# A two-layer decoder with divided tiles, and the score scale folded into the query weights

## Chip, core and metric

The kernel runs on one core of one Trainium2 chip. The metric is the device time of one execution in microseconds; the figure for a kernel is the median over its runs.

The engines are called as in the profile: PE (TensorE matmul; PEld is its weight load), DVE (VectorE), ACT (ScalarE), POOL (GpSimd) and SP (SyncE, which issues DMAs).

## What is computed

The input x is 64 sequences of 128 tokens of width 256, with a context of the same shape, all in float32. Two layers of three blocks each add to x; every block reads a layernorm of x:

```python
x = x + ssm(layernorm(x))                      # Mamba-like scan, convolution of 4, gate, rms norm
x = x + cross_attention(layernorm(x), ctx)     # 16 heads of 16, rotary, scale 0.25
x = x + recurrent_ffn(layernorm(x))            # c = f*c + i*g over the 64 sequences; tanh of x Wo + c_final Uo
x = x + self_attention(layernorm(x))           # rms norm, 16 query heads, 4 key heads, scale 1/16
x = x + wide_attention(layernorm(x), ctx)      # one head of 256, scale 1/16
x = x + experts(layernorm(x))                  # top 2 of 8 experts, and a shared expert
```

In each attention, `softmax(q k^T * scale) v`.

## The kernel before

**Tiling.** A group is G = 4 sequences, so T = 512 tokens; there are 16 groups. x stays in SBUF the whole time, one tile of 128 x 4 x 256 per group. The kernel has four stages, each with its own pools: stage 1 is the scan; stage 2 cross attention and the recurrence; stage 3 self attention, wide attention and routing; stage 4 the experts.

**Order.** Within a stage the work is written as Python generators, "tasks", with a start turn each. `run` advances every active task once per turn, oldest first, and a `yield` ends a task's turn. A group starts every 16 turns, an attention step (8 of the 16 heads of one sequence) every 2 turns. The tile framework then places the semaphores and fixes each engine's queue when the kernel is built. The trace shows that this queue isn't always in the order of the source: on DVE the instruction of L514 stands between those of L241 and L242.

**An attention step** (`heads`, L224 to L280). After two turns for the keys and values, two pairs of matmuls write the scores of 8 heads into a PSUM tile `s` (L236). DVE takes the maximum per head (L241) and multiplies it by minus the scale (L242), and ACT computes eight exponentials, `exp(scale*s - scale*max)`, into `e` (L245). Two turns later PE transposes the eight heads into a PSUM tile `pt` of two banks (L250). ACT copies the first four heads to `eT` (L252) and DVE the other four (L253). Two turns later the products with the values go to `av` (L261). Every second step ACT copies `av` out, PE transposes it back (L272), and DVE divides by the sums (L275, L277).

**Around it.** `block_diagonal` (L284, POOL) spreads the keys of four heads. `norm` computes the layernorm: statistics on DVE (L172 to L176), the power -0.5 on POOL (L163, `ln_rstd`) and the scaling on DVE (L189, `xn`). `transposed` (L200 to L204) transposes it through two PSUM tiles `pt_ln`; ACT copies the first half and DVE the second into one tile `xnT`. `project` (L211) and `project_rows` (L219) are the products with weights. In `cross_inputs` the rotary step writes `qT` and `kT` by halves (L512 to L519: PE, DVE, and two POOL instructions). The values `v` get a column block of ones from a POOL memset (L533, L669), so that the sums come out of the same product. The recurrence keeps its preactivations in `xg` (L577 to L607). `self_inputs` reads `xo` back from DRAM and adds it to x through POOL and ACT (L643 to L645). `route` writes its normalized, transposed x to DRAM (`XN`) for stage 4. POOL also scales some weights when they are loaded (`wout`, `fu`, `fuo`, `lwq`).

**PSUM in stages 2 and 3** (8 banks): three for `mm`, the tag of all short-lived products; two for `s`; two for `pt`; one for `av`.

The functions touched by the change, and what calls them:

Of the kernel before, what the change touches and what calls it, by code (L numbers as in the profile page):

```python
# [15 lines left out]
P = 128  # L16
# [46 lines left out]
def tile_decoder(ctx: ExitStack, tc: tile.TileContext, a: dict, out: bass.AP):  # L63
# [93 lines left out]
    nc.gpsimd.tensor_scalar_mul(fu, fu, 0.5)  # L157

# [35 lines left out]
    def transposed(work, ps, xn, bufs=2):  # L194

        xnT = work.tile([P, 2, T], F32, tag="xnT", name="xnT", bufs=bufs)
        for c in range(2):
            pt = ps.tile([P, T], F32, tag="mm", name="pt_ln")
            for b in range(G):
                nc.tensor.transpose(pt[:, b * P:(b + 1) * P], xn[:, b, c * P:(c + 1) * P], ident)  # L200
            if c == 0:
                nc.scalar.copy(xnT[:, c, :], pt)
            else:
                nc.vector.tensor_copy(xnT[:, c, :], pt)  # L204
        return xnT

    def project(ps, w, m0, m, rhs):

        o = ps.tile([P, T], F32, tag="mm", name="proj")
        for k in range(2):  # L210
            nc.tensor.matmul(  # L211
                o[:m, :], lhsT=w[:, k, m0:m0 + m], rhs=rhs[:, k, :], start=(k == 0), stop=(k == 1)
# [3 lines left out]
    def project_rows(dst, lhsT, w, b, m=None):  # L216

        for k in range(2):
            nc.tensor.matmul(  # L219
                dst, lhsT=lhsT[:, k, b * P:(b + 1) * P], rhs=w[:, k, :] if m is None else w[:, k, m],  # L220
# [3 lines left out]
    def heads(work, ps, b, c, state, q, kbd, v, scale):  # L224
# [9 lines left out]
        for hf in range(2):  # L234
# [4 lines left out]
            )  # L239
        mx = work.tile([P, 8], F32, tag="mx", name="mx", bufs=2)  # L240
        nc.vector.tensor_reduce(mx, s, AX.X, ALU.max)  # L241
        nc.vector.tensor_scalar(mx, mx, -scale, None, ALU.mult)  # L242
        e = work.tile([P, 8, P], F32, tag="e", name="e", bufs=2)
        for h in range(8):
            nc.scalar.activation(e[:, h, :], s[:, h, :], AF.Exp, bias=mx[:, h:h + 1], scale=scale)  # L245
        yield
        yield
        pt = ps.tile([P, 8, P], F32, tag="pt", name="pt")
        for h in range(8):
            nc.tensor.transpose(pt[:, h, :], e[:, h, :], ident)  # L250
        eT = work.tile([P, 8, P], F32, tag="eT", name="eT", bufs=2)
        nc.scalar.copy(eT[:, 0:4, :], pt[:, 0:4, :])  # L252
        nc.vector.tensor_copy(eT[:, 4:8, :], pt[:, 4:8, :])  # L253
# [6 lines left out]
        for vals, which, j, place in vh(c):  # L260
            nc.tensor.matmul(  # L261
                av[j * 32:j * 32 + 32, place, :], lhsT=vals, rhs=eT[:, which, :],
                start=True, stop=True,
            )
        if c == 1:
# [14 lines left out]
            state[b] = o  # L280

# [197 lines left out]
    for c in range(2):  # L479
        for w in (lwq, lwk, lwv):  # L480
            nc.gpsimd.tensor_scalar_mul(w[:, c, :], w[:, c, :], lg[:, c:c + 1])

# [7 lines left out]
    def cross_inputs(g, work, ps, got):  # L490
# [9 lines left out]
        for w, bias, src, tag in ((xwq, xbq, xnT, "qT"), (xwk, xbk, cT, "kT")):  # L500
            t = work.tile([P, 2, T], F32, tag=tag, name=tag, bufs=2)
# [8 lines left out]
            for c, raw in enumerate(raws):  # L510
                pr = ps.tile([P, T], F32, tag="mm", name="rot")
                nc.tensor.matmul(pr, lhsT=rot, rhs=raw, start=True, stop=True)  # L512
                tv = t[:, c, :].rearrange("p (b t) -> p b t", b=G)
# [6 lines left out]
            got[g, tag] = t  # L520
            yield
            yield
        got[g, "c"] = cT

    def cross_attention(g, b, c, work, ps, got):
        tb = slice(b * P, (b + 1) * P)

        def values():
            if c == 0:
                pv = ps.tile([P, T], F32, tag="mm", name="pv")  # L530
                project_rows(pv[:, :D], got[g, "c"], xwv, b)
                v = work.tile([P, 16, 32], F32, tag="v", name="v", bufs=3)
                nc.gpsimd.memset(v[:, :, 16:32], 1.0)  # L533
# [7 lines left out]
                (v[:, h, :], h % 8, h % 4, h // 4) for h in range(8 * c, 8 * c + 8)  # L541
# [3 lines left out]
            work, ps, b, c, got, got[g, "qT"][:, c, tb],  # L545
            lambda: block_diagonal(work, got[g, "kT"][:, c, tb]), values, 0.25,
# [18 lines left out]
    def recurrence(g, work, ps, got):  # L565
# [6 lines left out]
        xg = work.tile([P, 6, T], F32, tag="xg", name="xg")  # L572
        xo = work.tile([P, G, D], F32, tag="xo", name="xo")
        for part in range(2):
            for c in range(part * 3, part * 3 + 3):
                pp = project(ps, fx, c * P, P, xnT)
                nc.scalar.activation(xg[:, c, :], pp, AF.Identity, bias=fb[:, c:c + 1])  # L577
# [7 lines left out]
        for b in range(G):  # L585
            tb = slice(b * P, (b + 1) * P)
            c2 = got["c2"]
            for c0, n in ((0, 4), (4, 2)):
# [8 lines left out]
                pre = xg[:, c0:c0 + n, tb]  # L597
# [6 lines left out]
            nc.vector.scalar_tensor_tensor(kept, xg[:, 0:2, tb], 1.0, c2, ALU.add, ALU.mult)  # L604
            nc.vector.scalar_tensor_tensor(
                new, xg[:, 2:4, tb], 1.0, xg[:, 4:6, tb], ALU.add, ALU.mult
            )  # L607
# [600 lines left out]
```

## Time and profile before

| | |
|---|---|
| median of 3 runs | 3532.04 us (3531.86 to 3532.44) |
| profiled execution, its own time | 3483.77 us |
| its span | 3482.0 us |
| granted PE clock, mean | 0.948 |
| stage 1, to about | 784 us |
| stage 2, to about | 2000 us |
| stage 3, to about | 3050 us |
| one group in the steady part of stage 2 / stage 3 | 73 us / 57.6 us |

How to read the profile's lines. The trace is one execution. A line of a group gives source line, engine, operation, output and input with their shapes and the count; after the first bar the total busy time in us and the mean of one in ns; after the second bar the engine's idle time just before these instructions, with the engines and lines that ended it. A line of waits gives who waited for whom, the total in us, the number of times and the longest. A line of the timeline gives the start, the duration, the engine, and in brackets the idle time before it with what ended it. Idle time of an engine that doesn't bound the kernel costs nothing. The ends of PE's instructions are modelled, so a busy PE isn't necessarily a PE at its peak.

### The profile page before, as it was taken

The numbers are of one execution on the slowest core, as the hardware profiler recorded it, in microseconds if no ns is written. First come the engines' busy times: TensorE is split into PE (matmuls) and PEld (weight loads), VectorE is DVE, ScalarE is ACT, GpSimd is POOL, SyncE is SP. The second block draws the span as 40 slices with busy tenths as digits, with TensorE's granted clock in tenths as the row PEclk, the third lists the DMA queues.
The fourth block names the chain that finished last, engine by engine and source line by source line (L and its number), as shares of the span: only waits on it lengthen the run. The fifth ranks groups of instructions, "written<-read, shape, count | busy, mean of one in ns | idle before, by whom it ended". The sixth has DMA issues, their size and how long they took to land.

```text
span 3482.0 us, 48744 instructions
## 1 busy us (share of the span) xinstructions
PE 3176.3 (91%) x17486; PEld 2033.9 (58%) x17486; DVE 2273.2 (65%) x5498; ACT 1471.3 (42%) x3781; POOL 1302.8 (37%) x1290
## 2 busy tenths in 40 slices
PE   7899999998999999999999767999999999779989
PEld 4555555554666666666666633556566655468845
DVE  7999889965565556655565344777777777543355
ACT  3333333334545555455545234555555555213301
POOL 2444444455332323332332064233333333223276
PEclk9999999999999999999999878999998999789999
DMA  9980000001000000000000011101010101157655
GB/s 312 343 283 1 1 1 1 1 14 30 13 19 13 19 13 13 14 18 19 13 13 7 34 50 41 37 32 42 32 43 32 42 31 43 60 167 227 200 182 180
DMA packets 170658, 229.48 MB, mean 66 GB/s; under 512 B 19504, under 2 KB 142896, under 8 KB 170416
## 3 DMA queue, kind: packets, MB, share of 16 engines
q1 hardware_dynamic: 152448, 180.19, 16.0%
q0 software_dynamic: 17968, 46.18, 4.3%
q8 instruction: 138, 2.26, 0.3%
q14 instruction: 104, 0.85, 0.1%
HBM read 113.71 MB, written 127.93 MB: 69 GB/s over the span
## 4 chain that ended last, share of the span: by engine, by line
PE 62%; DVE 24%; POOL 6%; ACT 4%; DMA 2%; issue 2%; ACTq 0%; DVEq 0%; POOLq 0%; SPq 0%
PE proj L211 17%; PE pt L250 7%; PE s L236 6%; PE pu L593 5%; DVE acc L333 4%; DVE xn L189 4%; PE pgu L1019 4%; PE pv L219 3%; PE pt_ln L200 2%; PE av L261 2%; DVE mx L241 2%; PE pd L1028 2%; PE pxo L219 2%; PE pd L1079 1%; PE po L439 1%
## 5 line engine op out<-in xcount | busy, mean ns | idle before, releaser
L245 ACT ACTIVATE e<-s,mx 128x128 f32<-128x128 f32 x2048 | 555.9, 383 | 479.6 <-DVE mx L242 390.0
L284 POOL TENSOR_TENSOR kbd<-kT,consts 128x512 f32<-128x512 f32 x192 | 202.9, 1057 | 682.3 <-PE s L236 674.0
L253 DVE COPY eT<-pt 128x512 f32<-128x512 f32 x256 | 176.0, 687 | 392.7 <-ACT eT L252 391.7
L250 PE MATMUL pt<-consts,e 128*128 128x128 f32 x2048 | 362.5, 302 | 64.4 <-ACT e L245 62.6
L250 PEld LDWEIGHTS pt<-consts,e 128*128 128x128 f32 x2048 | 258.5, 148 | 180.8 <-ACT e L245 124.5
L211 PE MATMUL proj<-xnT,win 128*128 128x512 f32 x640 | 308.1, 621 | 48.9 <-DVE xc L323 45.0
L241 DVE TENSOR_REDUCE mx<-s 128x8 f32<-128x1024 f32 x256 | 310.5, 1213 | 10.0 <-PE s L236 9.9
L236 PE MATMUL s<-kbd,qT 64*128 64x512 f32 x1024 | 311.1, 686 | 1.5 <-POOL kbd L284 1.5
L252 ACT COPY eT<-pt 128x512 f32<-128x512 f32 x256 | 153.0, 598 | 191.7 <-PE pt L250 190.5
L211 PEld LDWEIGHTS proj<-xnT,win 128*128 128x128 f32 x640 | 119.9, 197 | 192.6 <-issue 112.6
L842 POOL DMA_INDIRECT xs<-xnr,r_rows x128 | 126.6, 989 | 271.5 <-DMA xs<-xnr,r_rows 183.8
L333 DVE SCALAR_TENSOR_TENSOR acc<-proj,convw,acc 128x508 f32<-128x508 f32 (+2 forms) x288 | 209.2, 730 | 7.7 <-ACT acc L329 6.2
L593 PEld LDWEIGHTS pu<-c,fu 128*128 128x128 f32 x1536 | 184.8, 196 | 24.9 <-issue 18.9
L593 PE MATMUL pu<-c,fu 128*128 128x128 f32 x1536 | 187.4, 280 | 8.9 <-DVE c L609 8.9
L392 POOL TENSOR_TENSOR ua<-consts,dt 128x1024 f32<-128x1024 f32 x64 | 121.9, 1906 | 179.7 <-DVE dt L366 150.6
L261 PE MATMUL av<-eT,v 128*32 128x128 f32 (+1 forms) x3072 | 174.5, 328 | 10.0 <-DVE eT L253 9.8
L211 PE MATMUL proj<-xnT,fx 128*128 128x512 f32 x384 | 173.4, 601 | 10.1 <-DVE v L534 9.6
L200 PE MATMUL pt_ln<-consts,xn 128*128 128x128 f32 x640 | 125.6, 316 | 61.5 <-DVE xn L189 39.5
L163 POOL TENSOR_TENSOR ln_rstd<-ln_ve,neghalf 128x4 f32<-128x4 f32 x96 | 98.0, 1021 | 210.4 <-DVE ln_ve L176 158.8
L189 DVE TENSOR_SCALAR xn<-x,ln_mv,ln_rstd 128x256 f32<-128x256 f32 x256 | 142.0, 600 | 40.4 <-POOL ln_rstd L163 40.4
L598 DVE TENSOR_TENSOR xg<-pu,xg 128x512 f32<-128x512 f32 (+1 forms) x128 | 71.4, 558 | 131.6 <-PE pu L593 131.6
L172 DVE BATCH_NORM_STATS2 ln_st<-x 128x6 f32<-128x256 f32 x384 | 146.3, 406 | 13.2 <-DMA x<-in_x_dram 6.2
(266 smaller groups left out, 6508.5 us busy)
## 6 DMA issues: line engine op xcount, KB each, us to landing
xs<-zeros SPq DMA_DIRECT2D x64, 1024.0 KB, 11.1
xs<-xs SPq DMA_DIRECT2D x71, 256.0 KB, 3.4
ys<-y SPq DMA_DIRECT2D x71, 256.0 KB, 2.3
ctxT<-in_ctxT_dram SPq DMA_DIRECT2D x32, 512.0 KB, 3.9
xo<-xo SPq DMA_DIRECT2D x32, 512.0 KB, 3.5
x<-in_x_dram SPq DMA_DIRECT2D x16, 512.0 KB, 8.9
xn<-xnT SPq DMA_DIRECT2D x16, 512.0 KB, 2.6
xnT<-xn SPq DMA_DIRECT2D x16, 512.0 KB, 4.6
```

Source lines behind the costliest of these rows:

```text
L189: nc.vector.tensor_scalar(xn[:, b, :], x[:, b, :], mv[:, b, 0:1], rstd[:, b:b + 1], ALU.subtract, ALU.mult)
L200: nc.tensor.transpose(pt[:, b * P:(b + 1) * P], xn[:, b, c * P:(c + 1) * P], ident)
L211: nc.tensor.matmul(o[:m, :], lhsT=w[:, k, m0:m0 + m], rhs=rhs[:, k, :], start=(k == 0), stop=(k == 1))
L236: nc.tensor.matmul(s[:, hf * 4:hf * 4 + 4, :], lhsT=q[rows], rhs=kb[rows, :, :], start=True, stop=True,)
L241: nc.vector.tensor_reduce(mx, s, AX.X, ALU.max)
L245: nc.scalar.activation(e[:, h, :], s[:, h, :], AF.Exp, bias=mx[:, h:h + 1], scale=scale)
L250: nc.tensor.transpose(pt[:, h, :], e[:, h, :], ident)
L253: nc.vector.tensor_copy(eT[:, 4:8, :], pt[:, 4:8, :])
L261: nc.tensor.matmul(av[j * 32:j * 32 + 32, place, :], lhsT=vals, rhs=eT[:, which, :], start=True, stop=True,)
L284: nc.gpsimd.tensor_tensor(out=kb, in0=mid(k, 4), in1=last(head, P), op=ALU.mult)
L333: nc.vector.scalar_tensor_tensor(acc[:, :, k:], pv[:, :, :P - k], convw[:, c, 3 - k:4 - k], acc[:, :, k:], ALU.mult, ALU.add,)
L593: nc.tensor.matmul(pu[:, i, :], lhsT=fu[:, k, c * P:(c + 1) * P], rhs=c2[:, k, :], start=(k == 0), stop=(k == 1),)
```

## The change

It has two parts.

1. **Tiles with two writers become two tiles.** `xnT`, `qT`, `kT` and `e`, `eT` are each split into two tiles; `pt` becomes two PSUM tiles of one bank, `pt0` and `pt1`; `xg` becomes a tile of 4 parts and one of 2. In `heads`, `tile_of` gives each head its place: heads 0, 1, 4, 5 go to the first tile and 2, 3, 6, 7 to the second, and the exponentials are issued in that order. The tiles `v` are allocated once (three in stage 2, two in stage 3), and the memset of their ones runs once each instead of once per sequence or group. `route` writes `xnT` with two DMAs instead of one.

2. **The scale and its sign move into weights.** POOL multiplies `xwq` and `xbq` by -0.25 and `lwq` by -1/16 once, when they are loaded. For the wide attention the ACT copies out of PSUM that produce `yu`, `ymb` and `ym` multiply by -1/16. The scores come out negated and scaled; the maximum becomes a minimum, used directly as the bias of `exp(-s + min)`. So the multiplications of L242 and L737 fall away.

The core of the diff:

```diff
     nc.gpsimd.tensor_scalar_mul(fu, fu, 0.5)
+    for w in (xwq, xbq):
+        nc.gpsimd.tensor_scalar_mul(w, w, -0.25)
...
-        xnT = work.tile([P, 2, T], F32, tag="xnT", name="xnT", bufs=bufs)
+        xnT = [work.tile([P, T], F32, tag=f"xnT{c}", name=f"xnT{c}", bufs=bufs) for c in range(2)]
...
         mx = work.tile([P, 8], F32, tag="mx", name="mx", bufs=2)
-        nc.vector.tensor_reduce(mx, s, AX.X, ALU.max)
-        nc.vector.tensor_scalar(mx, mx, -scale, None, ALU.mult)
-        e = work.tile([P, 8, P], F32, tag="e", name="e", bufs=2)
-        for h in range(8):
-            nc.scalar.activation(e[:, h, :], s[:, h, :], AF.Exp, bias=mx[:, h:h + 1], scale=scale)
-        yield
-        yield
-        pt = ps.tile([P, 8, P], F32, tag="pt", name="pt")
-        for h in range(8):
-            nc.tensor.transpose(pt[:, h, :], e[:, h, :], ident)
-        eT = work.tile([P, 8, P], F32, tag="eT", name="eT", bufs=2)
-        nc.scalar.copy(eT[:, 0:4, :], pt[:, 0:4, :])
-        nc.vector.tensor_copy(eT[:, 4:8, :], pt[:, 4:8, :])
+        nc.vector.tensor_reduce(mx, s, AX.X, ALU.min)
+
+        e, eT = (
+            [work.tile([P, 4, P], F32, tag=f"{n}{i}", name=f"{n}{i}", bufs=2) for i in range(2)]
+            for n in ("e", "eT")
+        )
+        for h in (0, 1, 4, 5, 2, 3, 6, 7):
+            i, at = tile_of(h)
+            nc.scalar.activation(
+                e[i][:, at, :], s[:, h, :], AF.Exp, bias=mx[:, h:h + 1], scale=-1.0
+            )
+        yield
+        yield
+        for i in range(2):
+            pt = ps.tile([P, 4, P], F32, tag=f"pt{i}", name=f"pt{i}")
+            for h in range(4):
+                nc.tensor.transpose(pt[:, h, :], e[i][:, h, :], ident)
+            if i == 0:
+                nc.scalar.copy(eT[i], pt)
+            else:
+                nc.vector.tensor_copy(eT[i], pt)
...
+    def tile_of(h):
+
+        return h % 4 // 2, h // 4 * 2 + h % 2
+
+    def values_of(work, n, i):
+
+        v = work.tile([P, n, 32], F32, tag=f"v{i}", name=f"v{i}")
+        nc.gpsimd.memset(v[:, :, 16:32], 1.0)
+        return v
...
+    nc.gpsimd.tensor_scalar_mul(lwq, lwq, -1.0 / 16)
...
-                v = work.tile([P, 16, 32], F32, tag="v", name="v", bufs=3)
-                nc.gpsimd.memset(v[:, :, 16:32], 1.0)
+                v = got["v"][(g * G + b) % 3]
...
-        xg = work.tile([P, 6, T], F32, tag="xg", name="xg")
+        xgs = [work.tile([P, n, T], F32, tag=f"xg{n}", name=f"xg{n}") for n in (4, 2)]
...
-        ps = PsumPool(psp, {"mm": 3, "s": 1, "pt": 1, "av": 1})
+        ps = PsumPool(psp, {"mm": 3, "s": 1, "pt0": 1, "pt1": 1, "av": 1})
...
-        nc.vector.tensor_reduce(mx, s, AX.X, ALU.max)
+        nc.vector.tensor_reduce(mx, s, AX.X, ALU.min)
 
         nc.vector.tensor_tensor(mx, mx, qb, ALU.add)
-        nc.vector.tensor_tensor(mx, qb, mx, ALU.subtract)
-        nc.vector.tensor_scalar(mx, mx, 1.0 / 16, None, ALU.mult)
+        nc.vector.tensor_tensor(mx, mx, qb, ALU.subtract)
...
-        nc.sync.dma_start(out=XN[g], in_=xnT)
+        for c in range(2):
+            nc.sync.dma_start(out=XN[g][:, c, :], in_=xnT[c])
...
-        nc.scalar.copy(yu, pb[:, :D + 1])
-        nc.scalar.copy(ymb, pb[:, D + 1:D + 3])
+        nc.scalar.mul(yu, pb[:, :D + 1], -1.0 / 16)
+        nc.scalar.mul(ymb, pb[:, D + 1:D + 3], -1.0 / 16)
...
-            nc.scalar.copy(ym[:, c, :], pw[:, :D])
+            nc.scalar.mul(ym[:, c, :], pw[:, :D], -1.0 / 16)
```

`qT`, `kT` and `xg` are divided in the same way, `halves` hands a whole tile on as a list of its two halves, and the pool of `work3` changes like that of `work2`.

## The prediction

> **What bounds the kernel now.** I read the page's busy shares first, then the stage windows, then who waits for whom on PE, and last the timeline of one loop period in each attention stage.
>
> ```profile
> PE 3176.3 (91%) x17486; PEld 2033.9 (58%) x17486; DVE 2273.2 (65%) x5498; ACT 1471.3 (42%) x3781; POOL 1302.8 (37%) x1290
> ```
>
> PE is busy 91% of the span, with 306 us idle. The change works mainly in stages 2 and 3, so their steady parts matter (columns: length, then busy time of PE, PEld, DVE, ACT, POOL; then granted clock, DMA share, GB/s):
>
> ```profile
> 870.00:1915.00 1045.00, 1004.88 (x6549) 656.36 (x6548) 613.91 (x1297) 536.67 (x1476) 336.41 (x326) 0.99 0.04 15
> 2176.00:2960.00 784.00, 749.94 (x4374) 468.50 (x4373) 584.74 (x1756) 410.75 (x1300) 256.94 (x279) 0.93 0.11 37
> ```
>
> PE is 96% busy in both. The whole pot is 40 us of PE idle in stage 2 (one group of four sequences takes 73 us, some 14 steady groups) and 34 us in stage 3 (57.6 us a group, some 14), plus matmuls stretched by a lower clock. PE's waits name their causes; first stage 2, then stage 3, steady part:
>
> ```profile
> PE pt_ln L200 <- DVE kT L514: 20.6, 14, 1.8
> PE proj L211 <- DVE v L534: 9.6, 11, 1.4
> PE pt L250 <- ACT e L245: 9.1, 13, 0.7
> ...
> PE pt L250 <- ACT e L245: 21.7, 16, 1.7
> ```
>
> So a wait comes about once per group and kind. By contrast, the largest waits that the change attacks sit on engines with slack:
>
> ```profile
> L245 ACT ACTIVATE e<-s,mx 128x128 f32<-128x128 f32 x2048 | 555.9, 383 | 479.6 <-DVE mx L242 390.0 <-DVE r_s L816 36.3 <-PE pr L557 33.3
> ...
> L253 DVE COPY eT<-pt 128x512 f32<-128x512 f32 x256 | 176.0, 687 | 392.7 <-ACT eT L252 391.7
> ...
> L242 DVE TENSOR_SCALAR mx<-mx 128x8 f32<-128x8 f32 x256 | 85.2, 333 | 2.7
> ```
>
> DVE's copy of its half of eT waits 392 us in all for ACT's copy of the other half, and the exponentials wait 390 us for L242. That is no gain as such: only what reaches PE counts. One stage 2 period shows how it does, first DVE's timeline, then ACT and PE:
>
> ```profile
> 1324.80 1.21 DVE L241 TENSOR_REDUCE mx<-s 128x8 f32<-128x1024 f32 x1
> 1325.94 0.67 DVE L514 TENSOR_TENSOR kT<-rot,consts 128x512 f32<-128x512 f32 x1
> 1326.54 0.76 DVE L242 TENSOR_SCALAR mx<-mx 128x8 f32<-128x8 f32 x1
> ```
>
> ```profile
> 1327.38 2.17 ACT L245 ACTIVATE e<-s,mx 128x128 f32<-128x128 f32 x8 [2.33 <-DVE mx L242]
> ...
> 1327.80 0.33 PE L250 MATMUL pt<-consts,e 128*128 128x128 f32 x1 [0.70 <-ACT e L245]
> ```
>
> The reduce is done at 1326.01, another group's kT comes between, L242 is stretched, and the exponentials start 1.37 us after the maxima were known. The queue's order isn't the source's: something was put between two lines that stand together. Stage 3's stall, on PE:
>
> ```profile
> 2443.55 2.13 PE L250 MATMUL pt<-consts,e 128*128 128x128 f32 x8 [1.39 <-ACT e L245]
> 2445.62 2.08 PE L236 MATMUL s<-kbd,qT 64*128 64x512 f32 x4
> ```
>
> L241 ended at 2442.84 there, L242 at 2443.04, and the exponentials began at 2443.13. After 1.39 us idle the eight transposes follow the exponentials one by one, and the scores take 2.08 us where other steps show 1.13.
>
> **What the Trainium skill says.** "TensorE: Matmul & The Clock Gate", Part 1: PE falls to half clock after an idle window of about 3.4 us. The trace agrees on the half: windows of 3.41 us from 2268.5 have clock 0.50. It doesn't agree that the window must be idle: PE was 2.70 of 3.41 us busy in the one before. "PSUM — Partial Sum Buffer", PSUM bank collisions: two engines must be kept apart in one bank, not in different banks. pt's halves lie in different banks, yet the trace shows DVE's copy starting at ACT's end, so the wait belongs to the shared tile, and separate tiles should free it. "SBUF — State Buffer", Who interferes with whom: a DVE tensor_scalar in its two-port mode and GpSimd exclude each other. L242 fits: median 170 ns, mean 333, longest 2304.
>
> **The change, part by part.** Gains are negative.
>
> *L242 goes (256 times, 85 us of DVE), with L737 (16 x 169 ns).* Stage 2: from 1326.67 to 1330.15 PE needs 3.48 us for 8 pt_ln, 8 pt and 2 pv. Undisturbed these advance by 0.92, 1.03 and 0.48 (other steps), 2.43 in all. The loss of 1.05 holds the 0.70 wait and the pace of the exponentials. With those at 1326.1 the loss is gone: 14 x 1.05 = -15. The waits for kT (1.44) and v (1.36) stay: L242 lies behind kT and v, not ahead. Stage 3: the exponentials could start at 2442.93 instead of 2443.13, but ACT's r_s at 2442.97, which waits for DVE too, may still stand ahead; of 0.2 I take 0.1. Less DVE work in this crowded stretch gives 0.2 more of the short waits after it (0.40 for r_sel, 0.27 for xnT): 14 x 0.3 = -4.
>
> *Clock.* 0.93 over 784 us means 14% of the time, 110 us, at half rate, which costs up to 55 us. Idle shrinks by 0.3 of the group's 2.2 us (14%; the 2.2 are 1.39 for e, the two short waits, and 0.14 for the wide attention's v), so -8. Stage 2: 0.99 costs at most 10; a third, -3. This term is the least sure: bounds 0 and -40 together.
>
> *e, eT and pt in two tiles each.* The eight exponentials, eight transposes and two copies remain. ACT's copy can start after four transposes (0.5 us sooner), DVE's at the eighth rather than after ACT's 0.58 us. av comes two turns later and waits for eT only 9.8 us in the span. Transposes already follow single exponentials, so dividing e gives nothing. In itself 0; DVE's copy leaving earlier is rival A.
>
> *xnT, qT, kT and xg divided.* L604 starts at 1311.94 while the second tanh on xg ends at 1312.49: parts of these tiles are already told apart. Bounds -3 and +3; 0.
>
> *v's memset (64 + 16 times, 0.31 us on POOL, waiting 143 us for av).* POOL's work behind it, kbd above all, waits for s anyway. v's DVE write takes over the wait, for reads of three sequences ago: done four turns before. Bounds -3 and +1; 0.
>
> *Weights scaled on POOL.* xwq is 128x512, like fuo's 1.54 us; xbq (128x2) is near dpar's 0.22 us. xwq lands at about 44 us (issued 34.6 to 36.1, 7.9 more), and POOL idles 15.4 us before 59.3. Hidden, unless queued ahead of the ua at 37.8: up to +6. lwq's 1.54 us falls at 794 to 802, where POOL runs without a break ahead of qT: +1.5. The wide attention's scale moves into ACT copies already there: 0.
>
> *route's DMA.* 16 more issues at 0.32 us on SP. XN is read in stage 4; SP is nearly idle: 0.
>
> *Ramps.* At 2029 to 2176 PE's exponential waits of 2 to 4 us come from the ring of xo (DMA 3.6, POOL 2.34, ACT 1.06, POOL 2.35), which isn't touched. Elsewhere about -3. Stages 1 and 4: no operation goes; 0.
>
> Sum: -15 - 4 - 8 - 3 + 1.5 - 3 = -31.5, taken as -32. The profiled execution has a span of 3482.0 and took 3483.8 us; the runs' median is 3532.0, 48 us more. I find nothing in the trace to split that 48, and carry the difference over: span 3450, median **3500**.
>
> **The rivals.** *A, eT's copy fills a hole.* DVE idles 1.06 us at 1321.1 and 1.13 us at 2438.6, waiting for POOL's ln_rstd, while eT is ready but for ACT. Its copy (0.60) then runs behind three xn. In the hole it would pull mx, kT and the exponentials 0.6 us ahead in both stages: (14 + 14 groups) x 0.6 = -17, and the clock gives 18 more, if a third of its 55 is tied to these stalls: 3500 - 35 = 3465. For it: on this chip the eighth transpose ends at 1321.45, in the hole. Against it: the order is fixed at build, and the copy would have to overtake three instructions, not one.
>
> *B, nothing reaches PE.* The stalls stay because DVE's other work (four xn, mx, kT) or ACT's r_s sets them, and only some 5 us come, from the ramps and the clock: 3527. The 0.70 wait, which has no cause but L242, speaks against it.
>
> *C, slower.* The new order puts DVE's eT copy, which needs the last transpose, ahead of work that frees a PSUM buffer, kT or v. All DVE work then stands behind it while PE is paced by the exponentials, about 2.2 us a period. 28 x 2.2 = +62, with 10 of clock: 3500 + 72 = 3572. It makes the change a loss from 32/28 = 1.1 us a group. For it: PE already waits for kT and v 27 times, so no slack is left there. Against it: the copy becomes ready earlier, not later.
>
> That the divided tiles free no wait is possible too; the sum has no gain from them, so it would end A and leave 3500.
>
> **How the numbers follow.** Forecast 0.52 (own range 3480 to 3520), A 0.23, B 0.10, C 0.15. Low takes in A with a better clock, 3445; high takes in B, the queued ua and a weak C, 3540. About 7 us, 0.2%, is what a measurement of this kernel can tell from no change: faster 0.75, same 0.10, slower 0.15.
>
> **What would show it.** Right: L242 gone and the exponentials waiting for L241; eT's DVE copy no longer waiting for ACT; PE's 9.1 us for e in stage 2 near zero while its 20.6 and 9.6 stay; stage 2 groups about 72 us; stage 3 clock 0.94 to 0.95. A: the waits for kT fall to half and the clock rises to 0.97. Wrong: a new wait on PE that recurs once a group, or a stage 1 that moves by more than 5 us.

## The result, and the profile after

| | before | changed |
|---|---|---|
| median of the runs | 3531.95 us (4 runs, 3530.0 to 3532.4) | 3503.61 us (4 runs, 3500.5 to 3511.0) |
| ratio | | 0.9924, 95% interval 0.9907 to 0.9941 |
| profiled execution, its own time | 3483.8 us | 3501.5 us |
| its span | 3482.0 us | 3499.7 us |

The changed kernel is 0.8% faster. The two profiled executions say the opposite, 3484 against 3501 us, so their spans can't be compared; parts of the kernel between fixed marks can. The marks are the starts of PE's first and last products with a weight (`xwq` opens stage 2, `fx` is the recurrence, `lwq` opens stage 3, `ym` is the wide attention), and of the last product with an expert's gate and up weights. A stage's ramp is the part before its groups come at a steady pace. In us:

| part | before | changed | difference |
|---|---|---|---|
| stage 1, to the first `xwq` | 791.6 | 792.5 | +0.9 |
| stage 2's ramp, to the first `fx` | 105.4 | 100.3 | -5.1 |
| stage 2, first to last `fx` | 1067.0 | 1052.2 | -14.8 |
| to the first `lwq` | 51.3 | 49.3 | -2.0 |
| stage 3's ramp, to the first `ym` | 140.9 | 125.8 | -15.1 |
| stage 3, first to last `ym` | 861.4 | 870.5 | +9.1 |
| to the last expert product | 287.3 | 289.0 | +1.7 |
| from there to the end | 177.1 | 220.1 | +43.0 |

Up to the last expert product the changed kernel gains 25.3 us, close to the 28 of the medians. The last row is a matter of the execution (experiment 0). The 0.9 us of stage 1 mean nothing: two executions of the kernel before differ by 4.5 us there (791.6 and 796.1). The ramp of stage 3 gains as much as all of stage 2, and the steady part of stage 3 loses.

The page's first line, and then the two stage windows, of the changed kernel:

```profile
PE 3183.3 (91%) x17486; PEld 2043.9 (58%) x17486; DVE 2233.7 (64%) x5226; ACT 1470.4 (42%) x3781; POOL 1286.1 (37%) x1218
```

```profile
870.00:1915.00 1045.00, 1016.99 (x6666) 663.51 (x6664) 594.42 (x1195) 549.67 (x1497) 316.05 (x267) 1.00 0.05 15
2176.00:2960.00 784.00, 753.33 (x4306) 474.05 (x4306) 567.12 (x1609) 405.28 (x1295) 254.94 (x265) 0.92 0.11 37
```

DVE has 272 instructions fewer (5498 before), which are the 256 of L242 and the 16 of L737, and POOL 72 fewer. In stage 2 PE is busy 1017 us of the 1045 instead of 1005, at clock 1.00 instead of 0.99, and it gets more done: 6666 products in the same 1045 us instead of 6549. In stage 3 the clock is 0.92 instead of 0.93, and the 784 us hold 4306 products instead of 4374 although PE is busy for longer. PE's waits, stage 2 first, then stage 3:

```profile
PE pt L263 <- ACT e L255: 14.0, 14, 2.8
PE proj L216 <- DVE v L558: 13.8, 13, 1.3
```

```profile
PE pt L263 <- ACT e L255: 30.3, 28, 2.1
```

In stage 2 the wait for kT, the largest of before (20.6 us), is gone; the waits for e and v remain and are larger than before (9.1 and 9.6). In stage 3 PE waits for e twice a group instead of once. But the waits of before for r_sel, eT and xnT (4.8, 3.1 and 1.7 us) shrink to 0.8 us for r_sel, so that all of PE's listed waits in stage 3 come to 31.6 us before and 31.4 after. The loss there isn't waiting. Part of it shows in the transposes of e, in the same window, first before, then changed (PE's busy time is the first number after the length, with its count):

```profile
2176.00:2960.00 784.00, 155.16 (x870) 113.09 (x870) 0.93 0.11 37
```

```profile
2176.00:2960.00 784.00, 165.09 (x856) 112.98 (x856) 0.92 0.11 37
```

That is 178 ns each before and 193 after, about 0.9 us for the 64 of a group: at the second stall they too follow the exponentials one by one, and the trace counts that as busy. The groups on the other engines:

```profile
L255 ACT ACTIVATE e<-s,mx 128x128 f32<-128x128 f32 x2048 | 557.4, 384 | 493.2 <-DVE mx L247 490.9
...
L267 DVE COPY eT<-pt 128x512 f32<-128x512 f32 x256 | 176.2, 688 | 337.3 <-PE pt L263 333.6
```

The exponentials now wait for the reduce itself (L247), and DVE's copy of eT for PE and no longer for ACT's copy. The timelines of DVE, ACT and PE in a stage 2 group, in that order:

```profile
1313.57 1.21 DVE L247 TENSOR_REDUCE mx<-s 128x8 f32<-128x1024 f32 x1
1314.71 1.27 DVE L539 TENSOR_TENSOR kT<-rot,consts 128x512 f32<-128x512 f32 x2
```

```profile
1314.88 2.18 ACT L255 ACTIVATE e<-s,mx 128x128 f32<-128x128 f32 x8 [3.97 <-DVE mx L247]
```

```profile
1313.79 0.64 PE L275 MATMUL av<-eT,v 128*32 128x128 f32 x16
1315.30 1.62 PE L263 MATMUL pt<-consts,e 128*128 128x128 f32 x6 [0.87 <-ACT e L255]
1316.76 0.27 PE L202 MATMUL pt_ln<-consts,xn 128*128 128x128 f32 x1
```

The exponentials start 0.10 us after the reduce ends (1314.78), where it was 1.37. And PE's own queue is another one. Before, two `pt_ln` stood ahead of the first transpose of e and waited 1.44 us for the PSUM buffer that kT held:

```profile
1326.67 0.44 PE L200 MATMUL pt_ln<-consts,xn 128*128 128x128 f32 x2 [1.44 <-DVE kT L514]
```

Now six transposes of e come first, and while they run kT is read. So the change has moved PE's order too, which is set when the kernel is built. With the scale alone (experiment 1) the six transposes stand first as well, with the tiles alone they don't: it is the instruction taken from DVE that changes the order on PE. The experiments ask which of these things pays.

### The profile page after: what moved, and what is told of

It is laid out like the page before. It is cut to its first block, busy times and chain, and to the rows that moved or that the text cites. A ratio compares the mean times of both kernels' runs of the same rounds, so it can differ in the third digit from the quotient of the medians.

```text
span 3499.7 us, 48489 instructions
## 1 busy us (share of the span) xinstructions
PE 3183.3 (91%) x17486; PEld 2043.9 (58%) x17486; DVE 2233.7 (64%) x5226; ACT 1470.4 (42%) x3781; POOL 1286.1 (37%) x1218
## 4 chain that ended last, share of the span: by engine, by line
PE 63%; DVE 22%; POOL 6%; issue 4%; DMA 2%; ACT 2%; another core or an unknown queue 1%; POOLq 0%; DVEq 0%; ACTq 0%; SPq 0%
PE proj L216 16%; PE pt L263 8%; PE s L241 6%; PE pu L619 5%; DVE acc L357 4%; PE pv L224 4%; DVE xn L191 3%; PE pgu L1046 3%; PE av L275 3%; PE pt_ln L202 3%; DVE mx L247 2%; PE pr L723 2%; PE pxo L224 2%; PE pd L1055 1%
## 5 line engine op out<-in xcount | busy, mean ns | idle before, releaser
L263 PEld LDWEIGHTS pt<-consts,e 128*128 128x128 f32 x2048 | 255.1, 147 | 192.8 <-ACT e L255 105.4
L216 PE MATMUL proj<-xnT,win 128*128 128x512 f32 x640 | 308.8, 622 | 48.1 <-DVE xc L347 45.1
L247 DVE TENSOR_REDUCE mx<-s 128x8 f32<-128x1024 f32 x256 | 311.9, 1219 | 62.5 <-PE s L241 61.9
L241 PE MATMUL s<-kbd,qT 64*128 64x512 f32 x1024 | 308.7, 681 | 1.2 <-POOL kbd L308 1.2
L265 ACT COPY eT<-pt 128x512 f32<-128x512 f32 x256 | 157.1, 614 | 119.0 <-PE pt L263 118.5
L216 PE MATMUL proj<-xnT,fx 128*128 128x512 f32 x384 | 172.3, 598 | 14.2 <-DVE v L558 13.8
L202 PE MATMUL pt_ln<-consts,xn 128*128 128x128 f32 x640 | 117.5, 320 | 43.5 <-DVE xn L191 42.5
L1070 POOL DMA_INDIRECT ys<-ys,t_yrow x128 | 123.8, 967 | 86.1 <-DVE x L1082 37.1
```

The source lines that it names most:

```text
L216: nc.tensor.matmul(o[:m, :], lhsT=w[:, k, m0:m0 + m], rhs=rhs[k], start=(k == 0), stop=(k == 1))
L241: nc.tensor.matmul(s[:, hf * 4:hf * 4 + 4, :], lhsT=q[rows], rhs=kb[rows, :, :], start=True, stop=True,)
L247: nc.vector.tensor_reduce(mx, s, AX.X, ALU.min)
L263: nc.tensor.transpose(pt[:, h, :], e[i][:, h, :], ident)
```

## The experiments

The stage times of all of them, as in the table above, in us ("sum" is from the first `xwq` to the last `ym`). Before's second profile agrees with its first within 0.8 us in all these parts but one, where it is 3.2 us off (and so is the sum); so differences of more than some 4 us in a part mean something although the totals scatter by 10 to 30. Each row is one profile. The ratios, not the medians, compare the kernels: each kernel ran beside runs of the kernel before, whose medians were 3533.7 to 3536.8 us in the experiments and 3532.0 in the result.

| kernel | ratio to before | stage 2 ramp | stage 2 | to `lwq` | stage 3 ramp | stage 3 | sum |
|---|---|---|---|---|---|---|---|
| before | 1 | 105.4 | 1067.0 | 51.3 | 140.9 | 861.4 | 2226.0 |
| 0 before again | | 105.7 | 1067.7 | 48.1 | 140.6 | 860.6 | 2222.7 |
| changed | 0.9924 | 100.3 | 1052.2 | 49.3 | 125.8 | 870.5 | 2198.1 |
| 1 scale only | 0.9909 | 102.3 | 1050.3 | 51.3 | 119.3 | 872.8 | 2196.0 |
| 2 tiles only | 0.9992 | 104.1 | 1061.1 | 51.3 | 139.2 | 863.3 | 2219.0 |
| 3 scale; e, eT, pt divided | 0.9945 | 100.5 | 1057.0 | 50.9 | 124.8 | 871.7 | 2204.9 |
| 4 changed; e, eT, pt whole | 0.9910 | 101.1 | 1048.5 | 49.5 | 120.4 | 872.1 | 2191.6 |
| 5 scale; x 1.0 in stage 3 | 0.9889 | 101.8 | 1052.4 | 49.6 | 118.5 | 866.1 | 2188.4 |
| 6 scale; x 1.0 aside | 0.9936 | 102.9 | 1050.9 | 49.4 | 120.1 | 872.6 | 2195.9 |
| 7 as 4; x 1.0 in stage 3 | 0.9896 | 101.2 | 1049.2 | 49.6 | 121.0 | 864.6 | 2185.6 |
| 8 scale; PE's order in stage 3 | 0.9936 | 101.4 | 1050.3 | 51.3 | 120.6 | 885.2 | 2208.8 |
| 9 scale; x 1.0 elsewhere | 1.0025 | 106.7 | 1066.7 | 48.1 | 140.0 | 864.9 | 2226.4 |
| 10 before; PE's order in stage 2 | 1.0051 | 106.0 | 1083.8 | 51.2 | 139.8 | 865.7 | 2246.5 |
| 11 as 4; PE's order in stage 3 | 0.9940 | 102.0 | 1048.3 | 49.6 | 119.4 | 883.4 | 2202.7 |

### 0. The kernel before, profiled again

No edit.

> The kernel before, unchanged, profiled once more. Its first profiled execution took 3483.8 us, its other runs 3532. Theory one, the 48 us lie in the tail: the experts end near 3300 us as they did (3299.8), and the part from there to the end takes about 230 us instead of 182. Theory two, they are spread over the stages: the experts end near 3345 us and the part after them takes about 182 us.

The time was 3539.4 us, and the last expert product fell at 3304.4 us (3304.9 in the first profile). Windows from about there to the end, first of before's first profile, then of its second:

```profile
3305.00:3482.00 177.00, 153.69 (x458) 87.22 (x456) 91.52 (x185) 18.27 (x31) 123.08 (x128) 0.96 0.59 180
```

```profile
3304.50:3537.50 233.00, 162.71 (x458) 92.88 (x456) 90.74 (x185) 18.05 (x31) 124.07 (x128) 0.86 0.44 137
```

The same 458 products and the same 128 gathers of experts' rows from DRAM took 177 and 233 us: in the second PE stands idle for 70 us instead of 23. Theory one holds: the 48 us that the prediction carried over lie in the output tail. The transfers themselves took no longer. The queue of the gathers, in the same two windows:

```profile
q0 software_dynamic: 6144, 16.79, 33.5%
```

```profile
q0 software_dynamic: 6144, 16.79, 24.6%
```

33.5% of 177 us are 59, and 24.6% of 233 are 57. So the added time lies between the transfers; what holds it up stays open. The changed kernel's profile has a tail of the usual kind (220 us; all profiles but before's first have 218 to 233).

### 1 and 2. The two halves of the change

The scale alone: in the kernel before, only the scaling in the weights and the minimum, with all tiles and memsets as they were (the wide attention's lines, changed likewise, are left out here).

```diff
+    for w in (xwq, xbq):
+        nc.gpsimd.tensor_scalar_mul(w, w, -0.25)
...
-        nc.vector.tensor_reduce(mx, s, AX.X, ALU.max)
-        nc.vector.tensor_scalar(mx, mx, -scale, None, ALU.mult)
+        nc.vector.tensor_reduce(mx, s, AX.X, ALU.min)
...
+    nc.gpsimd.tensor_scalar_mul(lwq, lwq, -1.0 / 16)
```

> The kernel before with only the scale moved into the weights (L242 and L737 go); every tile stays undivided and the memsets of v stay. Theory S, the removed DVE instruction carries the gain: 3505 to 3515 us, a stage 2 group at about 71.7 us instead of 72.95, and the experts end 15 to 25 us earlier. Theory T, the divided tiles carry it: 3525 to 3532 us, a stage 2 group within 0.3 us of 72.95.

The tiles alone are the changed kernel with these lines taken back:

> The changed kernel with the scale taken back (L242 and L737 are there again); all tiles are divided and v is static. Theory S: 3525 to 3535 us, a stage 2 group near 73 us. Theory T: 3500 to 3515 us, a stage 2 group near 71.7 us, and the wait of PE for kT gone as in the changed kernel. Both together: 3515 to 3520, each half of the 28 us.

Measured: the scale alone 3507.7 us, ratio 0.9909 (0.9891 to 0.9928); the tiles alone 3531.1 us, 0.9992 (0.9980 to 1.0005). Theory S holds in the total and in the place: the scale alone has the changed kernel's stage 2, its stage 3 ramp (somewhat shorter still) and its stage 3 loss. A group takes 71.71 us in stage 2 (median) and 58.8 in stage 3 (mean of ten groups), against 72.95 and 58.1 before; the 57.6 given for before at the top is too short for a mean. The tiles alone take 6 us off stage 2 and change each other part by 2 us or less. PE's waits in stage 2 of the scale alone, then of the tiles alone:

```profile
PE pt L251 <- ACT e L246: 18.8, 15, 1.7
PE proj L213 <- DVE v L536: 8.0, 13, 0.6
```

```profile
PE pt_ln L200 <- DVE kT L537: 16.0, 14, 2.9
PE pt L262 <- ACT e L254: 9.4, 14, 0.7
PE proj L214 <- DVE v L556: 8.3, 10, 0.9
```

The wait for kT goes with L242, not with the divided kT.

### 3 and 4. Which tiles

The scale, and of the tiles only e, eT and pt:

> The kernel before with the scale moved and only e, eT and pt divided; xnT, qT, kT and xg are whole and the memsets of v stay. If scale and attention tiles make the change, as both theories so far have it: 3500 to 3508 us, with stage 3's ramp near 126 us and a stage 3 group near 58.5 us as in the changed kernel. If the division of xnT, qT, kT and xg or the static v carries a part of it: 3515 us or more.

The opposite: the changed kernel with only these three made whole again.

```diff
-        for i in range(2):
-            pt = ps.tile([P, 4, P], F32, tag=f"pt{i}", name=f"pt{i}")
...
+        pt = ps.tile([P, 8, P], F32, tag="pt", name="pt")
+        for h in range(8):
+            nc.tensor.transpose(pt[:, h, :], e[:, h, :], ident)
+        eT = work.tile([P, 8, P], F32, tag="eT", name="eT", bufs=2)
```

> The changed kernel with e, eT and pt whole again; the scale in the weights, the divided xnT, qT, kT and xg and the static v stay. Stages 2 and 3 (first product with xwq to last with ym) took 2226.0 us before, 2198.1 in the changed kernel, 2196.0 with the scale alone, 2204.9 with the scale and divided e, eT, pt. If the effects add up, dividing e, eT and pt costs 9 us and the other divisions give 7: 2189 us here, and 3495 to 3500 in all. If dividing e, eT and pt is neutral and only moves PE's queue by chance: 2196 to 2200, and 3503 to 3508.

Measured: 3517.1 us, 0.9945 (0.9928 to 0.9961), so the other divisions carry a part; and 3500.7 us, 0.9910 (0.9895 to 0.9924), sum 2191.6 where 2189 was expected of effects that add up. They do, roughly, in the stages: with the other tiles whole, dividing e, eT and pt costs 8.9 us (2204.9 against 2196.0), with the others divided 6.5 (2198.1 against 2191.6); dividing the others and keeping v gives 4.4 to 6.8. These are sums from one profile each, which repeat to some 3 us, and in the totals the intervals of the changed kernel and of the one with e, eT and pt whole overlap. So the divided copy of eT, whose freed wait (392 us) is the largest that dividing tiles removes, brings nothing, and the three divided tiles together seem to cost a little. Why was not settled; in stage 2 the wait for v is larger with it (16.4 us against 8.0 in the scale alone).

### 5 and 6. The chain to the exponentials, or DVE's load

Experiment 6 puts DVE's 256 instructions back, but beside the chain; experiment 5 puts them into the chain in stage 3's steady groups alone.

```diff
         nc.vector.tensor_reduce(mx, s, AX.X, ALU.min)
+        side = work.tile([P, 8], F32, tag="side", name="side", bufs=2)
+        nc.vector.tensor_scalar(side, mx, 1.0, None, ALU.mult)
```

> The kernel with the scale alone, and at each step DVE multiplies the minima by 1.0 into a tile that nobody reads: as many DVE instructions as before, but none between the reduce and the exponentials. Theory chain: what counts is the shorter chain; stage 2 at 1050 to 1054 us, stage 3's ramp at 119 to 122, the total within 5 us of the scale alone. Theory load: DVE's 85 us of work count; stage 2 returns to 1060 or more, the total to within 10 us of the kernel before.

Measured: 3510.0 us, 0.9936 (0.9923 to 0.9948); stage 2 1050.9 us and the ramp 120.1, as without these instructions. The sum is 2195.9 us against 2196.0; the ratio is a little worse than that of the scale alone, with intervals that overlap (0.9891 to 0.9928). In the stages DVE's 85 us of work count for nothing; the place of L242 between the reduce and the exponentials is what counted. Experiment 5:

```diff
-    def heads(work, ps, b, c, state, q, kbd, v, scale):
+    def heads(work, ps, b, c, state, q, kbd, v, extra):
...
         nc.vector.tensor_reduce(mx, s, AX.X, ALU.min)
+        if extra:
+            nc.vector.tensor_scalar(mx, mx, 1.0, None, ALU.mult)
```

`extra` is true for `g >= 2` in `self_attention`, false in stage 2.

> The kernel with the scale alone, and in stage 3 from the third group on DVE multiplies the maxima by 1.0 between the reduce and the exponentials, as L242 stood there. Theory order: a shorter chain to the exponentials let the build put PE's transposes of e ahead of route's products; with the chain as long as before, a stage 3 group goes from 58.75 back to 58.0 us though DVE does more, the ramp of stage 3 stays near 119 us and stage 2 at 1050; 10 us less than the scale alone. Theory load: DVE work that is taken away can't make PE wait, the 0.75 us come from something else of the scale; a group stays at 58.7 or more, and the total rises by 0 to 5 us.

Measured: 3493.4 us, 0.9889 (0.9875 to 0.9904), a stage 3 group at 58.1 us. PE's waits in its stage 3 are before's again:

```profile
PE pt L253 <- ACT e L248: 19.8, 15, 1.7
PE pc L815 <- DVE r_sel L811: 4.9, 12, 0.4
```

That is what theory order forecast. With the chain short, ACT takes the eight exponentials ahead of r_s, a small activation of `route`, in 13 of 14 groups; with the longer chain r_s comes first. ACT's timeline in stage 3, first with the scale alone, then with the longer chain:

```profile
2414.61 2.17 ACT L246 ACTIVATE e<-s,mx 128x128 f32<-128x128 f32 x8
2416.62 0.28 ACT L792 ACTIVATE r_s<-r_s 128x32 f32<-128x32 f32 x1
```

```profile
2407.24 0.23 ACT L794 ACTIVATE r_s<-r_s 128x32 f32<-128x32 f32 x1
2407.40 2.17 ACT L248 ACTIVATE e<-s,mx 128x128 f32<-128x128 f32 x8
```

r_s ends 2 us later, DVE's route work behind it starts later and runs up to the next step's reduce, and PE has a second stall for e. But that stall isn't the loss: the tiles alone, with r_s first on ACT, have it too (27 waits, 26.0 us) with a group of 57.6 us. Experiments 8 and 9 show further that the order on PE or ACT doesn't settle the time.

### 7. The same with e, eT and pt whole

> The two together: e, eT and pt whole, all else of the change, and in stage 3 from the third group on DVE's multiplication by 1.0 between the reduce and the exponentials. If the effects add up: 10 us less than the kernel without that multiplication, 3485 to 3492 in all, and a stage 3 group near 57.5 us (it was 57.66 with all tiles divided and L242 kept). If they don't: within 3 us of it.

Measured: 3493.6 us, 0.9896 (0.9881 to 0.9910), a stage 3 group at 57.9 us, sum 2185.6. That is 7 us less in the total than experiment 4, with overlapping intervals, and 6 less in the stages; it lies between the two forecasts (10 less, or within 3). Experiments 5 and 7 are the fastest of these kernels, about 10 us under the changed one; only for experiment 5 the intervals don't overlap.

### 8 and 11. PE's order alone, in stage 3

Nothing is computed otherwise; an edge of order, without a semaphore, keeps the first transpose of e behind route's second product.

```diff
+        hold[:] = [nc.tensor.matmul(pcv[:, 1], lhsT=ones, rhs=sel, start=True, stop=True)]
...
+            made = nc.tensor.transpose(pt[:, h, :], e[:, h, :], ident)
+            if h == 0 and hold:
+                tc.add_manual_dep(
+                    made.ins, hold.pop().ins.name,
...
```

> The kernel with the scale alone, with no instruction added: PE's queue alone is changed, so that in stage 3 the first transpose of an attention step's e can't stand ahead of route's second product pc when pc was issued first. Theory order: as with the multiplication by 1.0, but with less DVE work; a stage 3 group at 57.6 to 58.1 us instead of 58.75, stage 2 at 1050 and the ramp at 119 as with the scale alone, 3488 to 3496 us in all. Rival, what helped was the later start of the exponentials itself (ACT free for route's activation): a group stays at 58.7.

> The changed kernel with e, eT and pt whole, and PE's queue in stage 3 held in the order of before (pc ahead of the next step's transposes). If the effects add up: stages 2 and 3 (first product with xwq to last with ym) at 2180 to 2186 us instead of 2198.1 in the changed kernel, 3485 to 3493 us in all, the fastest of these kernels.

Measured: 3515.0 us, 0.9936 (0.9920 to 0.9953), and 3514.9 us, 0.9940 (0.9920 to 0.9959). Both missed: stage 3 takes 885 and 883 us, some 12 more than with PE's order left alone, and a group of experiment 8 takes 59.7 us. PE's waits in its stage 3:

```profile
PE pc L823 <- DVE r_sel L819: 27.5, 14, 2.3
PE pt L253 <- ACT e L248: 17.6, 15, 1.7
```

The second stall has moved from e to r_sel and grown. ACT still had r_s behind the exponentials there (2414.34 and 2416.35), and r_sel came no earlier. So in these two kernels PE's new order suited ACT's new order, and setting PE's queue back alone cost time. Whether r_s ahead of the exponentials on ACT alone would pay was not tried.

### 9. The longer chain in the other places

As experiment 5, with `extra` true in all of stage 2 and for `g < 2` in stage 3.

> The kernel with the scale alone, with the multiplication by 1.0 between the reduce and the exponentials in all of stage 2 and in the first two groups of stage 3, where the chain was said to help. If the chain's length is all that the scale changes: stage 2 back to 1067 us, stage 3's ramp back to 140, the steady part stays at 872; 3540 us or a little more, slower than before by some 7. If the ramp's 21 us have another cause (the scaling of lwq on POOL, the phase in which stage 3 begins): the ramp stays below 130.

Measured: 3545.3 us, 1.0025 (1.0015 to 1.0035). Stage 2 is back at 1066.7 us and the ramp at 140.0: the whole gain of both hangs on that one place in the chain, with the queues that the build makes of it. What the ramp does is seen in ACT's timeline, first of before, then of the changed kernel:

```profile
2035.36 1.06 ACT L644 ACTIVATE xo<-xo 128x1024 f32<-128x1024 f32 x1 [6.78 <-POOL xo L643]
2036.33 2.15 ACT L245 ACTIVATE e<-s,mx 128x128 f32<-128x128 f32 x8
```

```profile
2012.13 2.18 ACT L255 ACTIVATE e<-s,mx 128x128 f32<-128x128 f32 x8 [4.51 <-DVE mx L247]
2014.14 0.64 ACT L265 COPY eT<-pt 128x512 f32<-128x512 f32 x1
2014.63 1.11 ACT L669 ACTIVATE xo<-xo 128x1024 f32<-128x1024 f32 x1
```

Before, each step's exponentials stand behind a tanh of the xo ring, which comes about every 10 us: from the first `lwq` on, 14 tanhs start before the first `ym`. In the changed kernel the first step's stand ahead of the second tanh, as shown, and later two steps fit into one period; 12 tanhs pass. Two periods are about 20 us; 15.1 were gained, 21.6 with the scale alone (12 tanhs too).

The surprise is stage 3: 864.9 us where 872 was expected, though the steady groups of experiments 1 and 9 have the same instructions in the same order on PE, ACT, DVE and POOL, and PE waits for e as often:

```profile
PE pt L253 <- ACT e L248: 27.0, 27, 1.3
```

Windows of one group each, first four of the changed kernel, then three of experiment 9 (the clock is the third column from the end):

```profile
2482.90:2542.80 59.90, 58.00 (x327) 36.65 (x325) 43.51 (x124) 30.22 (x96) 19.89 (x21) 0.89 0.11 36
2542.80:2601.50 58.70, 56.35 (x326) 35.34 (x324) 42.65 (x123) 30.11 (x96) 18.93 (x21) 0.94 0.11 37
2601.50:2660.10 58.60, 55.98 (x327) 35.39 (x325) 43.40 (x123) 30.22 (x96) 19.33 (x21) 0.94 0.11 37
2660.10:2718.40 58.30, 56.39 (x326) 35.40 (x324) 42.53 (x122) 30.15 (x96) 19.00 (x21) 0.91 0.11 37
```

```profile
2460.40:2518.60 58.20, 56.24 (x327) 35.34 (x325) 42.71 (x123) 30.50 (x96) 19.57 (x22) 0.91 0.11 37
2518.60:2575.90 57.30, 55.33 (x327) 34.05 (x325) 42.53 (x123) 30.49 (x96) 19.58 (x22) 0.94 0.11 38
2575.90:2634.30 58.40, 56.45 (x327) 35.59 (x325) 42.25 (x123) 30.50 (x96) 19.41 (x22) 0.91 0.11 37
```

In the changed kernel every fourth group takes 59.8 us at clock 0.89, and this repeats (59.8, 58.7, 58.6, 58.3, 59.8); in experiment 9 every third takes 57.3. So this loop runs in one of two cycles, of 58.9 us (235.5 / 4) or 58.0 us (173.9 / 3) a group, and the same queues are found in both: experiment 9 itself begins with a group of 59.8 us and then changes over.

What differs from group to group is the time for which PE's clock stands at half rate. In the clock records of both kernels each group has its half-rate time in the same part, from some 45 us after its first product with `ym`. It is one stretch of 13.65 us in the groups of 59.8 us and one of 6.83 us in the groups of 57.3; the groups between have 10.24 us, or two stretches of 3.41 us.

Before and experiment 5 have no group of 59.8 us, but one of 57.1 to 57.5 among every two to four. This goes, for the most part, with the order on ACT. The kernels with r_s ahead of the exponentials (before, experiments 2, 5, 7 and 10) take 57.6 to 58.1 us a group; those with r_s behind (the changed one, experiments 1, 3, 4, 6, 8 and 11) take 58.6 to 59.7, but experiment 9, with r_s behind too, takes 58.2. So the order goes with longer groups in seven of eight kernels but doesn't force them, and the 6.7 us by which experiment 5's stage 3 is shorter can't be put down to it alone. What selects the cycle is open.

### 10. PE's order alone, in stage 2

The kernel before, where the same kind of edge puts the recurrence's `pt_ln` behind the sixth transpose of e.

```diff
+                if after and recent:
+                    tc.add_manual_dep(
+                        made.ins, recent[5].ins.name,
...
+        recent[:] = [nc.tensor.transpose(pt[:, h, :], e[:, h, :], ident) for h in range(8)]
```

> The kernel before, L242 in place and nothing of the change made; in stage 2 PE's queue alone is changed: the recurrence's pt_ln can't stand ahead of the sixth transpose of the step that was issued before it, as in the changed kernel. Theory order: the wait for kT is gone, the one for e grows to what L242 adds (1.3 + 0.3 to 0.8 us), a group at 71.8 to 72.4 us instead of 72.95, stage 2 at 1054 to 1061. Theory latency: the exponentials are as late as before, so PE only waits elsewhere; a group at 72.8 to 73.5, stage 2 at 1066 or more.

Measured: 3556.8 us, 1.0051 (1.0032 to 1.0070), slower; a group takes 73.86 us and stage 2 1083.8. PE's waits in stage 2:

```profile
PE pt L262 <- ACT e L258: 36.0, 14, 2.6
PE proj L224 <- DVE v L546: 0.9, 5, 0.2
```

The wait for kT is gone, but the one for e is up to 2.6 us long: L242 still holds the exponentials behind kT on DVE, and all the transposes wait for them. Theory latency's 1066 us or more holds; its group length is missed by 0.4 us. Yet waiting isn't what makes it slower: these waits sum to 36.9 us, less than before's 39.3. What has changed for the worse is the clock:

```profile
870.00:1915.00 1045.00, 1007.81 (x6480) 661.15 (x6478) 588.22 (x1287) 532.89 (x1459) 335.40 (x325) 0.97 0.04 15
```

The granted clock is 0.97 where before has 0.99. By estimate, 0.02 of 1045 us are up to 20 us, enough for the 16.8 us by which stage 2 is longer. Why the clock fell was not tried; PE's idle time has come together in one long wait a group. So the order on PE, with the exponentials as late as before, doesn't pay. The short chain with PE's old order was not tried, so how the 15 us of stage 2 divide between the two stays open.

## Why the prediction was right, and where not

The forecast of 3500 us and its case hold: 3503.6, from the chain between L241 and the exponentials, in the change's scale part. That it came so close is in part luck: two terms were far off, in opposite ways. Term by term:

- **L242 in stage 2, with the clock, -15 and -3: measured -14.8.** The size is near. PE's waits went from 39.3 to 27.8 us (20.6 + 9.6 + 9.1 to 14.0 + 13.8), -11.5; the rest is busy time, at a clock of 1.00 instead of 0.99. The mechanism is only half right. "The waits for kT (1.44) and v (1.36) stay" was wrong, and so was the test put beside it, e near zero while 20.6 stays: the wait for kT went, those for e and v grew. The step that failed is the assumption that each queue keeps its order and only loses an instruction. That the build sets an order across the source had been seen on DVE; it wasn't carried to PE.
- **L242 in stage 3 with its clock, -4 and -8: measured +9.1.** This is the worst term. The step that failed is that less DVE work makes the short waits shorter and leaves the rest as it was: a second stall for e appeared, once a group, which the prediction had named as a sign of being wrong, and PE's waits stayed at 31 us in all. Nor did the clock rise to 0.94 or 0.95; it was 0.92, and the loop had gone into the slower of two cycles. What selects it is open.
- **Ramps, -3, the xo ring "isn't touched": measured -5.1 and -15.1.** The ring isn't touched, but the exponentials that stood behind its tanh on ACT were let ahead of it. The failing step is again a fixed order on a queue.
- **Divided tiles, 0: right in sum, +2 us in the stages beside the scale alone.** It consists of +6.5 to +9 for e, eT and pt and -4 to -7 for the others; on the kernel before the tiles give -7 in the stages and nothing that the totals show. Rival A, the copy of eT in a hole, is excluded: the copy no longer waits for ACT, and nothing is gained by it. In stage 2's group it stands after the first of the four xn and not in the hole.
- **Weights, DMAs, stages 1 and 4, 0 to +1.5: right within what can be told.** `xwq` is scaled at 44.1 us in 1.54 us and nobody waits for it; `lwq` takes 1.49 us at 798.9, and nobody is listed as waiting.
- **The 48 us: right to carry them over.** One profile couldn't place them; the second puts them into the output tail.
- **Rival B, nothing reaches PE.** Excluded by experiments 1 and 9, which differ by the instruction in this chain alone and by 41 us of PE's time.
- **Rival C, slower.** Not this change. Experiment 10 is slower by 0.9 us a group through an order alone, though on PE and not, as C had it, on DVE, and with a lower clock rather than with more waiting.

The two large errors nearly cancel: +21 us in stage 3 (-12 forecast, +9 measured) and -17 in the ramps (-3 and -20). The sum of -32 stands against -25 in the stages and -28 in the medians for that reason too, not only because stage 2 was sized well.

## What to carry to other kernels

An instruction's worth isn't its duration but its place in the chain to the engine that bounds: in this kernel DVE's multiplications cost nothing in the stages beside the chain, and 41 us in it, in stage 2 and the first two groups of stage 3 (experiments 1 and 9: 1271.9 and 1313.4 us for stage 2, its ramp and stage 3's). Where the build orders the queues, taking one instruction out can reorder several engines at once, as it did here, so read the new queues stage by stage before trusting the old waits; setting the order of one of them alone made its stage 11 to 17 us slower in each of three kernels. Don't take PE's waits for the whole loss: in stage 3 and in experiment 10 they stayed or fell while the time rose. Compare parts between fixed marks in the trace, not spans, where a tail varies by 50 us, as it did here.

## What was not expected of the hardware

- **The clock's windows and the loop seem to lock together.** In stage 3 the stretches at half rate are 3.41, 6.83, 10.24 or 13.65 us long in the trace's clock records, multiples of the same 3.41 us. The cycle of four groups lasts 235.5 us, 69.0 of these, the cycle of three 174.0 us, 51.0, and experiment 8's cycle of two 119.5 us, 35.0. So the same instructions take 0.9 us a group more or less, by estimate about 13 us over some 14 groups. The Trainium skill, "TensorE: Matmul & The Clock Gate", Part 1, has a free-running window of 3413 ns, which agrees; that a loop settles into whole numbers of it is seen in these three cycles alone.
- **The output tail varies from one execution to another, and not by slower transfers.** The same 128 gathers and products took 177 and 233 us in two executions of one kernel, while the gathers' transfers took 59 and 57.
- **A small DVE instruction can last until a POOL instruction ends.** L242 takes 170 ns in the median, but 52 of its 256 took over 500 ns, 48 us of its 85. Of these, 51 ended 25 to 39 ns after an instruction on POOL that was running when they began; in the stage 2 period of the prediction (0.76 us) that is POOL's L518. So part of what L242 cost in the chain was time in which POOL's instruction ran.
